# A two-layer Perceiver kernel on one core: which PSUM banks attention, state space preparation and gate of layer 1 use, and two batches' attention outputs in one tile

## The chip, the cores and the metric

The kernel runs on one core of a Trainium2 chip. A core has a matrix engine (TensorE, PE in the profile; its weight loads are PEld), a vector engine (VectorE, DVE), an activation engine (ScalarE, ACT), a general engine (GpSimd, POOL) and a queue that issues transfers (SyncE, SP). They run side by side, each through its own instruction list in a fixed order, and wait for one another by semaphores. Matrix results go to PSUM, which this kernel divides into eight banks of 128 partitions by 512 float32 values.

The metric is the device time of one execution in microseconds. Before the change it is 2087.88 us, the median of three runs (2087.57 to 2094.29).

## The reference

64 sequences of 32 tokens of width 256 attend to 64 contexts of 257 rows of width 256 and go through two layers:

```
x = x + L0_xattn(layernorm(x), ctx)     # attention over the context
x = x + L0_attn(layernorm(x))           # a recurrence (RWKV) and a channel mix
x = x + L0_ffn(layernorm(x))            # 8 experts, two chosen by gates
x = x + L1_xattn(layernorm(x), ctx)     # grouped attention, quantized linear maps
x = x + L1_attn(layernorm(x))           # a selective state space model
x = x + L1_ffn(layernorm(x))            # 8 experts, all summed
```

The change touches the fourth line and the fifth, and through shared banks the sixth. Attention of layer 1 has 16 query heads and 8 key heads of 16:

```
q = bit_linear(x, wq);  k = bit_linear(y, wk);  v = bit_linear(y, wv)
attn = softmax(q k^T / 4);  out = layernorm(attn v);  return bit_linear(out, wo)
```

`bit_linear` normalizes rows, rounds them to 8 bits and multiplies by weights of -1, 0 or 1 with a scale. The state space model is

```
xz = x @ in_proj.T + b;  x_main, z = split(xz)
xc = silu(causal_conv(x_main));  ssm = xc @ x_proj.T + b     # B (16), C (16), delta
h = exp(A dt) * h + dt * B * xc;  y = <h, C> + D * xc         # step by step
out = layernorm((y * silu(z)) @ out_proj.T + b + x)
```

## The kernel before

The 2048 tokens are cut into four blocks (0 to 3) of 512 tokens, which is 16 sequences; a block has four query tiles of 128 tokens, that is of four sequences ("batches") of 32. Each layer part is a stage, a Python function that emits the instructions of one block. `_stage0`, `_stage1` and `_stage2` are layer 0; `_stage3` is attention of layer 1; `_stage4` the state space model, in three functions `ahead` (preparation), `gates` (the silu of z) and `recur` (the recurrence); `_stage5` the experts of layer 1. `layers` (lines 1195 to 1254) calls them in an order in which blocks overlap: beside `recur(b)` of block b stand attention of block b+1 and experts of block b-1. A scheduler below the kernel then puts the instructions of each engine into one fixed list, guided by the order of calling and by its own estimate of times; it also decides which buffer of a pool a tile gets, when the tile is first used.

**The PSUM pools.** While layer 1 runs, the banks are shared out like this: `k.ps` (tag "s") two banks for attention, `k.psh` two for the recurrence (`h`, `outps`), `k.psp` (tag "p") one for preparation and gate, `k.psu` (tag "u") one for the experts' `up`, `t_ps`, `lg_ps` and `rT`, and two which first belong to the experts of layer 0 and then to the sums `acc` of the experts of layer 1. A tile that needs a bank waits until every reader of the bank's last tile is done. Attention of block 0 is called before the pools `psh`, `psp` and `psu` are opened (lines 1225 and 1230).

**Attention, one query tile** (`attend`, line 766). The quantized queries are transposed (`xqT_ps`, L776, copied at L778), multiplied by the weights (`q_ps`, L781, scaled on VectorE at L783), and transposed again (`qT_ps`, L800) into `qm` (L804), which has one buffer. `last_ps` (L787, L789) and `sl_ps` (L807) treat the 257th context row. Then the four batches go in pairs (e = 0 and 2):

- `keys(e)`: `kT_ps` (L823) and `v_ps` (L830) for two batches, evacuated and scaled on VectorE (L825, L836).
- `scores(e, h0)`: for two head pairs at a time two tiles `sc` (L844), their negated maxima `nm` on VectorE (L849, L851), exponentials on ScalarE (L855) with sums.
- `sums(e)`: for one batch, two tiles `pt_ps` of four transposes each (L868), copied on ScalarE (L870), then 16 small matmuls into `oT_ps` (L878). Its two halves are masked and added into `od` by ScalarE (L882) and VectorE (L883).
- `back()`: the weights of the sums (`rt_ps` L904), the output transposed (`po_ps` L916, VectorE L918) and the 257th row added (`vl_ps` L920, L922, GpSimd L923).

`block` (line 703) interleaves them: `keys(e)`, `scores(e, 0)`, then `sums` of both batches of the pair before, then `scores(e, 2)`. All these tiles take turns in the two banks of `k.ps`. At the block's end stand a layer norm (L743, L744 on GpSimd), quantization (L344 to L350), and for each query tile `yqT_ps` (L758) and `wo_ps` (L763), which is added into x at L764.

**State space model.** `ahead` normalizes x, transposes it (`tps`, L123), projects each of four channel groups (`inps`, L976) to ScalarE (L994, L997) and VectorE (L1001, the convolution), then `ssm_ps` (L1012), whose rows go to DRAM and come back broadcast to all partitions (L1016, L1018); softplus gives dt (L1022 to L1030). `gates` has four more `inps` tiles with a silu (L1038). `recur` has for each of 16 states and four channel groups an exponential on ScalarE (L1060), a scan on VectorE (L1061) and a product (L1062); GpSimd makes the scan's inputs (L1056) and adds up y (L1063) for two groups at once, multiplies by the gate (L1066) at the end; then `outps` (L1074).

**Experts of layer 1.** For each of 8 experts: four `up` tiles (L1167) with their evacuation (L1169), one gelu (L1171), and matmuls into `acc` (L1175). Weights are loaded by SyncE (L1162, L1163) into two buffers. The two `acc` tiles leave at L1180, are transposed (`rT`, L1187) and scaled (L1188). In the order of TensorE the experts of one block begin with `t_ps` (L1121) and the gate logits `lg_ps` (L1126).

The small helpers by which the stages take their banks:

```
700    def ps(shape, name, dt=F32):                     # attention
701        return k.ps.tile(shape, dt, name=name, tag="s")
967    def pp(shape, name):                             # preparation and gate
968        return k.psp.tile(shape, F32, name=name, tag="p")
1102   def ps(shape, name):                             # experts
1103       return k.psu.tile(shape, F32, name=name, tag="u")
```

Of the kernel before, what the change touches and what calls it, by code (L numbers as in the profile page):

```python
# [70 lines left out]
def _chan(k, name, j=0):  # L71
    at = CHAN_AT[name] + j
    return k.chan[:, at : at + 1]
# [595 lines left out]
def _stage3(k, w, tmp):  # L669
# [30 lines left out]
    def ps(shape, name, dt=F32):  # L700
        return k.ps.tile(shape, dt, name=name, tag="s")

    def block(b):
        xs = [k.x[b][:, j, :] for j in range(4)]
# [16 lines left out]
        for u in range(9):  # L721
            j, e = divmod(2 * u, 4)
            if u < 8:
                if e == 0:
                    tiles[j] = attend(4 * b + j, j, xq, dq, o4)
                tiles[j].keys(e)
                tiles[j].scores(e, 0)
            if u:
                last, le = tiles[(u - 1) // 2], (2 * u - 2) % 4
                last.sums(le)  # L730
                last.sums(le + 1)
            if u < 8:
                tiles[j].scores(e, 2)
            if u and le == 2:
                last.back()
# [30 lines left out]
    def attend(g, j, xq, dq, o4):  # L766
# [6 lines left out]

        xqT_ps = ps([P, 2, P], "xqT_ps", BF16)
        for c in range(2):
            nc.tensor.transpose(xqT_ps[:, c, :], xq[:, j, c * P : (c + 1) * P], k.identb)  # L776
        xqT = k.wk3.tile([P, 2, P], BF16, name="xqT", tag="xqT")
        nc.scalar.copy(xqT, xqT_ps)  # L778
        q_ps = ps([P, D], "q_ps")
        for c in range(2):  # L780
# [3 lines left out]

        last_ps = ps([P, P + 4], "last_ps")
        for c in range(2):
# [10 lines left out]
        )  # L797
        qT_ps = ps([P, 2, 4, T], "qT_ps")
        for h in range(2):
# [3 lines left out]
        for l in range(2):  # L803
            nc.vector.tensor_scalar(qm[:, :, l].rearrange("p e n g -> p g e n"), qT_ps, half[:, l : l + 1], None, ALU.mult)  # L804
        sl_ps = ps([P, 4, 4], "sl_ps")
        for e in range(4):
# [11 lines left out]
        def keys(e):  # L818


            kT_ps = ps([P, 2, 2 * P], "kT_ps")
            for c in range(2):
                nc.tensor.matmul(kT_ps, wkv[:, c, 0:P], cq[:, c, e : e + 2, 0 : 2 * P], start=c == 0, stop=c == 1)  # L823
            kTs[e] = k.wk3.tile([P, 2, 2 * P], F32, name="kT", tag="kT")
            nc.vector.tensor_tensor(kTs[e], kT_ps, kb[:, e : e + 2, 0 : 2 * P], ALU.mult)  # L825
            v_ps = ps([P, 2, 2, P], "v_ps")
            for m in range(2):
                for f in range(2):
                    for c in range(2):
                        nc.tensor.matmul(  # L830
                            v_ps[:, m, f, :], cq[:, c, e + f, m * P : (m + 1) * P], wkv[:, c, P : 2 * P],
                            start=c == 0, stop=c == 1,
                        )
            vs[e] = k.wk3.tile([P, 2, 2, P], F32, name="v", tag="v")
            cd = k.cdq[:, :, g].rearrange("p (m e) -> p m e", m=2)[:, :, e : e + 2]
            nc.vector.tensor_tensor(vs[e], v_ps, cd.unsqueeze(3).to_broadcast([P, 2, 2, P]), ALU.mult)  # L836
# [23 lines left out]
        def sums(e):  # L860
            e0, f = e - e % 2, e % 2
            pts = []
            for hp in range(2):

                pt_ps = ps([P, 2, 2, P], "pt_ps")
                for h in range(2):
                    for m in range(2):
                        nc.tensor.transpose(pt_ps[:, h, m, :], ws[e0, hp][:, f, h, m * P : (m + 1) * P], k.ident)  # L868
                pt = k.wk3.tile([P, 2, 2, P], F32, name="pt", tag="pt")
                nc.scalar.copy(pt, pt_ps)  # L870
                pts.append(pt)

            oT_ps = ps([P, 2, 2 * T], "oT_ps")
            ob = oT_ps.rearrange("p l q -> p (l q)")
            for m in range(2):
                for h in range(4):
                    r = slice(32 * h, 32 * h + 32)
                    nc.tensor.matmul(  # L878
                        ob[r], vs[e0][:, m, f, r], pts[h // 2][:, h % 2, m, :],
                        start=m == 0, stop=m == 1, skip_group_check=True,  # L880
                    )
            nc.scalar.activation(od4[:, e], oT_ps[:, 0], AF.Copy, scale=half[:, 0:1])  # L882
            nc.vector.scalar_tensor_tensor(od4[:, e], oT_ps[:, 1], half[:, 1:2], od4[:, e], ALU.mult, ALU.add)  # L883

# [49 lines left out]
def _stage4(k, w, wk):  # L934
# [32 lines left out]
    def pp(shape, name):  # L967
        return k.psp.tile(shape, F32, name=name, tag="p")

# [64 lines left out]
    def gates(v):  # L1034

        v.zs = wk.tile([P, C, BT], F32, name="zs", tag="zs", bufs=1)
        for c in range(C):
            nc.scalar.activation(v.zs[:, c, :], project(v, C + c, pp), AF.Silu, bias=_chan(k, "L1_attn_in_proj_b", C + c))  # L1038

# [155 lines left out]
def layers(k, out):  # L1195
# [140 lines left out]
```

## Time and profile before

| what | value |
|---|---|
| time, median of 3 runs | 2087.88 us |
| the profiled execution's own time | 2087.24 us |
| its span, first to last instruction | 2085.2 us |
| TensorE busy | 1597.6 us (77%) |
| VectorE busy | 1384.2 us (66%) |
| GpSimd busy | 1049.5 us (50%) |
| ScalarE busy | 944.1 us (45%) |
| granted TensorE clock, mean | 0.832 |

The span in 40 equal slices of 52 us, each digit the busy share of an engine in tenths (9 is 90% or more), below them the clock that TensorE was granted in tenths of full speed:

```profile
PE   4776967667979788657387789877888787787798
DVE  4588585765485568888777888775787844877100
ACT  2454352303445264434136466447566536564232
POOL 5344646413121324668724677732677843999100
PEclk9676968778989989657697789988699997899799
```

Layer 0 fills the slices up to about the ninth, with attention of block 0 up to the fourteenth. The runs of 8 in VectorE's row with 6 to 7 in GpSimd's are recurrence and attention beside each other; the dips between them are preparations. The run of 9 in GpSimd's row is the last recurrence, and the last three slices are experts alone.

In the views shown later a group of instructions is told by line, engine, operation, tiles ("out<-in"), shape and count. A row of the timeline starts with the start and the duration in us and ends, in brackets, with the idle time of the engine before it and what ended it; a row of the waits names who waited for whom, the total in us, the times and the longest.

### The profile page before, as it was taken

What the parts mean: (1) busy time and instruction counts of PE and PEld (TensorE: products, weight loads), DVE (VectorE), ACT (ScalarE), POOL (GpSimd) and SP (SyncE); (2) the same over time, 40 slices, a digit from 0 to 9 for tenths busy, and PEclk for the clock granted to TensorE, in tenths of its full rate; (3) what the DMA queues carried; (4) which work ended last, traced back from release to release, by engine and by line L of the source; (5) the groups of instructions that cost most, each with busy time, mean ns of one, the idle gap of its engine ahead of it and who ended that gap; (6) DMA issues with size and microseconds to landing.
All of it is one profiled execution on the core that took longest, in us unless ns stands there. A gap on an engine that the chain in (4) does not pass through costs nothing. (4 is left out here: it accounts for less than half of the span.)

```text
span 2085.2 us, 20012 instructions
## 1 busy us (share of the span) xinstructions
PE 1597.6 (77%) x6323; PEld 812.4 (39%) x6323; DVE 1384.2 (66%) x2443; ACT 944.1 (45%) x2001; POOL 1049.5 (50%) x1069
## 2 busy tenths in 40 slices
PE   4776967667979788657387789877888787787798
PEld 3333534334545434433144344433344433233343
DVE  4588585765485568888777888775787844877100
ACT  2454352303445264434136466447566536564232
POOL 5344646413121324668724677732677843999100
PEclk9676968778989989657697789988699997899799
DMA  6754333300001010122002232102222212342121
GB/s 221 228 189 141 102 109 104 100 4 21 21 21 42 20 47 21 51 59 63 10 15 83 66 106 86 46 21 87 71 81 71 52 31 77 87 115 72 39 81 41
DMA packets 88376, 151.23 MB, mean 73 GB/s; under 512 B 7740, under 2 KB 52300, under 8 KB 86224
## 3 DMA queue, kind: packets, MB, share of 16 engines
q1 hardware_dynamic: 85428, 148.75, 23.4%
q10 hardware_dynamic: 2844, 1.22, 0.2%
q8 instruction: 50, 0.82, 0.2%
q14 instruction: 54, 0.44, 0.1%
HBM read 139.03 MB, written 10.92 MB: 72 GB/s over the span
## 5 line engine op out<-in xcount | busy, mean ns | idle before, releaser
L1056 POOL TENSOR_TENSOR g<-dtx,bc 128x1024 f32<-128x1024 f32 x128 | 300.4, 2352 | 191.4 <-DVE h L1061 101.7
L1061 DVE TENSOR_TENSOR_SCAN h<-h,g 128x512 f32<-128x512 f32 x256 | 308.1, 1219 | 47.0 <-ACT h L1060 28.7
L1063 POOL TENSOR_TENSOR xc<-xc,hc 128x1024 f32<-128x1024 f32 x128 | 301.0, 2354 | 34.5 <-DVE hc L1062 29.5
L1167 PE MATMUL up<-xT,w 128*128 128x512 f32 x512 | 288.4, 678 | 33.1 <-ACT hid L1169 29.6
L1175 PE MATMUL acc<-hid,w 128*128 128x512 f32 x512 | 258.0, 624 | 19.9 <-ACT hid L1171 19.9
L1060 ACT ACTIVATE h<-dt,A 128x512 f32<-128x512 f32 x256 | 173.9, 692 | 173.5 <-DVE hc L1062 172.3
L1062 DVE TENSOR_TENSOR hc<-h,bc 128x512 f32<-128x512 f32 x256 | 170.1, 681 | 5.8 <-POOL xc L1063 3.0
L1169 ACT ACTIVATE hid<-up,chan 128x512 f32<-128x512 f32 x128 | 87.2, 681 | 179.2 <-PE up L1167 179.2
L855 ACT ACTIVATE p<-sc,nm 128x256 f32<-128x256 f32 x256 | 117.7, 471 | 95.3 <-DVE nm L851 90.5
L1167 PEld LDWEIGHTS up<-xT,w 128*128 128x128 f32 x512 | 97.7, 209 | 157.3 <-issue 84.6
L630 PE MATMUL weps<-we,xT 128*128 128x512 f32 x256 | 140.0, 671 | 23.3 <-DVE x L632 14.7
L868 PE MATMUL pt_ps<-ident,p 128*128 128x128 f32 x512 | 95.9, 325 | 73.6 <-ACT p L855 36.3
L1175 PEld LDWEIGHTS acc<-hid,w 128*128 128x128 f32 x512 | 96.5, 199 | 137.8 <-issue 99.3
L844 PE MATMUL sc<-kT,qm 32*128 32x256 f32 x512 | 133.9, 447 | 4.9 <-DVE kT L825 2.4
L849 DVE TENSOR_REDUCE nm<-sc 128x2 f32<-128x512 f32 x128 | 86.2, 686 | 56.1 <-PE sc L844 55.1
L868 PEld LDWEIGHTS pt_ps<-ident,p 128*128 128x128 f32 x512 | 67.3, 163 | 123.0 <-ACT p L855 79.1
L89 POOL TENSOR_TENSOR rs_t<-rs_r 128x4 f32<-128x4 f32 (+3 forms) x138 | 33.3, 243 | 160.4 <-DVE rs_r L87 142.5
L844 PEld LDWEIGHTS sc<-kT,qm 32*128 32x128 f32 x512 | 82.7, 207 | 62.6 <-issue 10.8
L1188 DVE SCALAR_TENSOR_TENSOR o<-rT,gt,x 128x256 f32<-128x256 f32 x16 | 7.7, 483 | 133.2 <-PE rT L1187 124.0
L870 ACT COPY pt<-pt_ps 128x512 f32<-128x512 f32 x128 | 74.2, 588 | 32.9 <-PE pt_ps L868 32.3
L1044 POOL TENSOR_TENSOR dtx<-xc,dt 128x2048 f32<-128x2048 f32 x4 | 18.0, 4502 | 138.9 <-DVE dt L1030 127.4
L247 POOL TENSOR_TENSOR cT<-cT,scb 128x2056 f32<-128x2056 f32 x16 | 73.2, 4572 | 25.8 <-PE scT_ps L237 11.5
(389 smaller groups left out, 3166.0 us busy)
## 6 DMA issues: line engine op xcount, KB each, us to landing
bc<-rows SPq DMA_DIRECT2D x64, 512.0 KB
w<-in_L_ffn_w_dram SPq DMA_DIRECT2D x64, 512.0 KB
cT<-in_ctxT_dram SPq DMA_DIRECT2D x16, 1028.0 KB
cq<-cq SPq DMA_DIRECT2D x32, 514.0 KB
cn<-in_ctx_dram SPq DMA_DIRECT2D x64, 256.0 KB
scb<-scales SPq DMA_DIRECT2D x16, 514.0 KB
kb<-steps SPq DMA_DIRECT2D x16, 514.0 KB
x<-in_x_dram SPq DMA_DIRECT2D x4, 512.0 KB
```

The costliest lines, as they stand in the source:

```text
L630: nc.tensor.matmul(ps, xT[:, c, r], we[:, c, e : e + 2, :], start=c == 0, stop=c == 1)
L844: nc.tensor.matmul(sc[h][:, f, :], qm[r, e + f].rearrange("p l n g -> p (l n g)"), kTs[e][r, f, :], start=True, stop=True,)
L855: nc.scalar.activation(w_[:, f, h - h0, :], sc[h][:, f, :], AF.Exp, bias=nm[:, e + f, h : h + 1], accum_out=sm[:, e + f, h : h + 1],)
L868: nc.tensor.transpose(pt_ps[:, h, m, :], ws[e0, hp][:, f, h, m * P : (m + 1) * P], k.ident)
L1056: nc.gpsimd.tensor_tensor(g, dtx[:, c2 : c2 + 2], bc[:, 0:1, :].to_broadcast([P, 2, BT]), ALU.mult)
L1060: nc.scalar.activation(h, dt, AF.Exp, scale=A[:, c2 + c, n : n + 1])
L1061: nc.vector.tensor_tensor_scan(h, h, g[:, c, :], 0.0, ALU.mult, ALU.add)
L1062: nc.vector.tensor_tensor(hc[:, c, :], h, bc[:, 1, :], ALU.mult)
L1063: nc.gpsimd.tensor_tensor(y[:, c2 : c2 + 2], y[:, c2 : c2 + 2], hc, ALU.add)
L1167: nc.tensor.matmul(u, w1[e][:, c, q * P : (q + 1) * P], xT[:, c, :], start=c == 0, stop=c == 1)
L1169: nc.scalar.activation(hid[e][:, q, :], u, AF.Identity, bias=b1)
L1175: nc.tensor.matmul(acc[o], w2[e][:, q, o * P : (o + 1) * P], hid[e][:, q, :], start=n == H, stop=n == E * H + H - 1)
```

## The change

Four things change.

1. A helper `pk` takes a tile from `k.psp` (one bank) if that pool is open, else from `k.ps`. The tiles `xqT_ps`, `q_ps`, `last_ps`, `qT_ps`, `sl_ps`, `kT_ps` and `v_ps` of attention use it. `k.psp` is set to None before block 0, so block 0 keeps them in `k.ps`.
2. `sums(e)` treats both batches of a pair. They share one tile `oT_ps` in one bank, and one instruction of ScalarE and one of VectorE, on twice the columns, move both to `od`.
3. The preparation `ahead` takes its tiles (`tps`, `inps`, `ssm_ps`) from the two banks of `k.ps`.
4. `gates` takes its tiles from the experts' bank `k.psu`.

```diff
+    def pk(shape, name, dt=F32):
+        return k.psp.tile(shape, dt, name=name, tag="p") if k.psp else ps(shape, name, dt)
...
                 last.sums(le)
-                last.sums(le + 1)
...
-        xqT_ps = ps([P, 2, P], "xqT_ps", BF16)
+        xqT_ps = pk([P, 2, P], "xqT_ps", BF16)
...
-        q_ps = ps([P, D], "q_ps")
+        q_ps = pk([P, D], "q_ps")
...
-        last_ps = ps([P, P + 4], "last_ps")
+        last_ps = pk([P, P + 4], "last_ps")
...
-        qT_ps = ps([P, 2, 4, T], "qT_ps")
+        qT_ps = pk([P, 2, 4, T], "qT_ps")
...
-        sl_ps = ps([P, 4, 4], "sl_ps")
+        sl_ps = pk([P, 4, 4], "sl_ps")
...
-            kT_ps = ps([P, 2, 2 * P], "kT_ps")
+            kT_ps = pk([P, 2, 2 * P], "kT_ps")
...
-            v_ps = ps([P, 2, 2, P], "v_ps")
+            v_ps = pk([P, 2, 2, P], "v_ps")
...
         def sums(e):
-            e0, f = e - e % 2, e % 2
-            pts = []
-            for hp in range(2):
-                pt_ps = ps([P, 2, 2, P], "pt_ps")
...
-            oT_ps = ps([P, 2, 2 * T], "oT_ps")
-            ob = oT_ps.rearrange("p l q -> p (l q)")
...
-            nc.scalar.activation(od4[:, e], oT_ps[:, 0], AF.Copy, scale=half[:, 0:1])
-            nc.vector.scalar_tensor_tensor(od4[:, e], oT_ps[:, 1], half[:, 1:2], od4[:, e], ALU.mult, ALU.add)
+            oT_ps = ps([P, 2, 2, 2 * T], "oT_ps")
+            for f in range(2):
+                pts = []
+                for hp in range(2):
+                    pt_ps = ps([P, 2, 2, P], "pt_ps")
...
+                ob = oT_ps[:, f].rearrange("p l q -> p (l q)")
...
+            o2 = od4[:, e : e + 2]
+            nc.scalar.activation(o2, oT_ps[:, :, 0], AF.Copy, scale=half[:, 0:1])
+            nc.vector.scalar_tensor_tensor(o2, oT_ps[:, :, 1], half[:, 1:2], o2, ALU.mult, ALU.add)
...
     def pp(shape, name):
-        return k.psp.tile(shape, F32, name=name, tag="p")
+        return k.ps.tile(shape, F32, name=name, tag="s")
+
+    def pz(shape, name):
+        return k.psu.tile(shape, F32, name=name, tag="u")
...
-            nc.scalar.activation(v.zs[:, c, :], project(v, C + c, pp), AF.Silu, bias=_chan(k, "L1_attn_in_proj_b", C + c))
+            nc.scalar.activation(v.zs[:, c, :], project(v, C + c, pz), AF.Silu, bias=_chan(k, "L1_attn_in_proj_b", C + c))
...
+    k.psp = None
     with left0:
```

The matmuls and the transfers are the same in number and size; 32 instructions of ScalarE and 32 of VectorE go (64 of each become 32, of twice the columns). The scheduler makes new instruction lists for every engine.

More of the change, by code (lines that the diff above doesn't have):

```diff
@@ L860, in sums @@
         def sums(e):
-            e0, f = e - e % 2, e % 2
-            pts = []
-            for hp in range(2):
-                pt_ps = ps([P, 2, 2, P], "pt_ps")
[L866 to L871, printed above, removed]
-            oT_ps = ps([P, 2, 2 * T], "oT_ps")
-            ob = oT_ps.rearrange("p l q -> p (l q)")
[L875 to L883, printed above, removed]
+            oT_ps = ps([P, 2, 2, 2 * T], "oT_ps")
[3 more added lines that the diff above has]
+                    pt_ps = ps([P, 2, 2, P], "pt_ps")
+                    for h in range(2):
+                        for m in range(2):
+                            nc.tensor.transpose(pt_ps[:, h, m, :], ws[e, hp][:, f, h, m * P : (m + 1) * P], k.ident)
+                    pt = k.wk3.tile([P, 2, 2, P], F32, name="pt", tag="pt")
+                    nc.scalar.copy(pt, pt_ps)
+                    pts.append(pt)
+                ob = oT_ps[:, f].rearrange("p l q -> p (l q)")
+                for m in range(2):
+                    for h in range(4):
+                        r = slice(32 * h, 32 * h + 32)
+                        nc.tensor.matmul(
+                            ob[r], vs[e][:, m, f, r], pts[h // 2][:, h % 2, m, :],
+                            start=m == 0, stop=m == 1, skip_group_check=True,
+                        )
+            o2 = od4[:, e : e + 2]
+            nc.scalar.activation(o2, oT_ps[:, :, 0], AF.Copy, scale=half[:, 0:1])
+            nc.vector.scalar_tensor_tensor(o2, oT_ps[:, :, 1], half[:, 1:2], o2, ALU.mult, ALU.add)
         def back():
```

## The prediction

> **What bounds the kernel now.** I read the table of forty slices first: no engine is full for long, and what is busy changes with the stage. So I cut the span where a query block's attention ends (last L764), where a recurrence starts (first L1061) and where it ends (last L1074), and took the view of busy time by stretch:
>
> ```profile
> core 0: us, PE busy (x) PEld busy (x) DVE busy (x) ACT busy (x) POOL busy (x), PEclk, DMA share, GB/s
> 792.00:1044.00 252.00, 150.92 (x748) 84.82 (x748) 213.47 (x350) 92.79 (x243) 170.34 (x114) 0.67 0.16 42
> 1120.00:1378.00 258.00, 207.68 (x880) 103.90 (x880) 207.55 (x328) 142.14 (x290) 177.96 (x134) 0.84 0.22 67
> 1451.00:1691.00 240.00, 192.70 (x818) 95.85 (x819) 187.46 (x300) 131.76 (x274) 174.97 (x133) 0.84 0.22 62
> 1752.00:1923.00 171.00, 132.24 (x290) 56.37 (x290) 137.70 (x161) 94.84 (x120) 156.01 (x84) 0.89 0.30 83
> 1923.00:2086.00 163.00, 138.00 (x320) 60.62 (x318) 13.69 (x47) 47.75 (x52) 12.83 (x44) 0.89 0.18 55
> ```
>
> The first three rows are attention of blocks 1, 2, 3 beside the recurrence of blocks 0, 1, 2 (and, from 1120 on, experts of blocks 0 and 1): VectorE is busy 78 to 85%, TensorE 60 to 80%, neither full. The fourth is the last recurrence, where GpSimd is busy 91% (156.0 of 171). The fifth is experts alone, bound by TensorE. Between the rows stand the state space preparations (1044 to 1120, 1378 to 1451, 1691 to 1752). The chain of waits agrees for the end (its largest entries are experts' matmuls L1175 and L1167) but reaches back only to 1648 us, so for the middle I read waits. VectorE's, from 792 to 1691 us:
>
> ```profile
> DVE nm L849 <- PE sc L844: 41.4, 36, 4.7
> DVE od L883 <- ACT od L882: 18.8, 7, 10.0
> DVE h L1061 <- ACT h L1060: 15.2, 16, 5.3
> DVE kT L825 <- PE kT_ps L823: 14.5, 10, 3.9
> ```
>
> VectorE is idle 197 us of these 899 (701.9 busy), and three of the four largest waits are for attention's PSUM tiles. Why these are late, the timeline shows where one query tile ends and the next begins:
>
> ```profile
> 1511.21 0.48 ACT L855 ACTIVATE p<-sc,nm 128x256 f32<-128x256 f32 x1
> ...
> 1513.81 0.28 PE L776 MATMUL xqT_ps<-identb,xq 128*128 128x128 bf16 x2
> ...
> 1517.80 0.46 DVE L783 TENSOR_SCALAR q<-q_ps,dq 128x256 f32<-128x256 f32 x1
> ...
> 1520.32 0.95 PE L807 MATMUL sl_ps<-klm,qm 128*128 128x4 f32 x8
> ...
> 1522.98 1.89 PE L844 MATMUL sc<-kT,qm 32*128 32x256 f32 x6
> ```
>
> From the last exponential (done 1511.8) to the next scores (1523.0) are 11.2 us in which queries and keys pass through the two banks that scores and transposes also need.
>
> **The change, part by part.** Sums are made against the profiled execution: span 2085.2, its own time 2087.24, so 2.0 us lie around the span; it stands 0.6 below the median of 2087.88. Where instructions go I take from the order of both built programs, engine by engine; no time comes from there.
>
> *Queries and keys in their own bank.* It holds for blocks 1 to 3; block 0 runs before the bank exists. In the new order the next tile's xqT and q stand before the scores' end, and keys of the second half tile right behind those of the first. So the 11.2 us shrink to what the order forces (qm has one buffer, so L804, sl and kT still follow the last scores): 0.9 + 1.0 + 0.6 + 0.7 by their rows and a VectorE turn or two of 1.2 us (L1061), some 5 us, beside the exponentials. At the half tile 4.2 us (1545.2 to 1549.4) lose the keys' 2.5. That takes 8 to 9 us off attention's chain per query tile, some 100 us for twelve. Most of it cannot be cashed: recurrence shares VectorE, whose work between landmarks is the same in both orders (from the first to the last scan 822 us before, 818 after, by mean durations). Only idle time can go, and of it what waits for attention's tiles: 41.4 + 18.8 + 14.5, with q, v and qm (1.9, 2.8, 1.5) 80.9 us. Ends: none of it, all of it. I take half, since nm will still wait for some scores: **-40**.
>
> *One output tile for two batches.* L882 and L883 run half as often on twice the columns. Rows: L882 0.31 us at 64 columns, L855 0.47 at 256, so about 0.36 at 128; L883 0.28, L918 0.41, so about 0.32. For the 24 pairs of blocks 1 to 3, VectorE saves 24 x (0.56 - 0.32) = 6 us. The fourth transpose group no longer waits for L883 of the first batch but for the copy L870 (0.6 us) in the one bank that the output leaves free; the tile is taken only at its first matmul, so the first two groups still have two banks. Beside the waits already counted: **-4** (ends 0 and -6). Block 0 gets this too, but from 480 to 713 us TensorE idles only 31 of 233 us: nothing, from -6 to +6.
>
> *Preparation in two banks, gate in the experts' bank.* Before, each inps tile waits for its eviction, and experts fill in between. After, the four stand in a row. The matmuls from the last wo (L763) to the last ssm (L1012) come, by mean durations per line, to 35.4, 38.3, 36.7 us for blocks 1, 2, 3 before and 32.3, 34.5, 31.1 after; block 3's interval is 34.3 us in the trace (1690.1 to 1724.4), so TensorE sets it. **-12** (0 to -18 with block 0's -5.8). The gate's four tiles of a block now take turns with the experts' up tiles; both orders finish a gate before the experts of the block after it, and y needs it only at L1066. ScalarE loads four tables fewer (4 x 1.28 us), covered by its slack (ScalarE busy 50% from 792 to 1691): 0. The rows and dt loads stand before the expert weights that would block SyncE's queue (w1 and w2 of expert 7 of the block then running), so it is not stalled.
>
> *What is moved.* The experts lag. Of block 2's 128 expert matmuls (each two passes), 13 stand behind the last outps before (2 up, 11 acc), **54** after (22 and 32). The recurrence covered them; in the tail nothing does:
>
> ```profile
> 1928.68 7.13 PE L1175 MATMUL acc<-hid,w 128*128 128x512 f32 x16 [2.28 <-ACT hid L1171]
> ...
> 1948.96 3.58 PE L1126 MATMUL lg_ps<-w_L_ffn_gate_wT,xT 128*128 128x8 f32 x16 [0.68 <-ACT xT L1122]
> 1952.83 3.78 PE L1167 MATMUL up<-xT,w 128*128 128x512 f32 x4 [0.28 <-DVE lg L1136]
> ...
> 1966.51 1.98 PE L1167 MATMUL up<-xT,w 128*128 128x512 f32 x4 [0.78 <-ACT hid L1169]
> ```
>
> Block 3's experts begin only when block 2's output has left (single bank, single xn5 buffer), 17 us after the last acc (1935.8 to 1952.5). So 41 x 0.86 us (four passes in 1.72 in the steady part of the chain) = **+35** go in whole; ends +30 and +40.
>
> *The clock.* 1953 to 1966 us ran at a granted 0.51, after 13 us of thin work; then 1.00. The Trainium skill (TensorE: Matmul & The Clock Gate, Part 1) says that idleness halves the clock and that some 3.4 us of work restore it; here 13 us were needed. By that rule, taking experts' matmuls out of the attention stretches speaks against the change: without experts the clock was 0.67 (792 to 1044), with them 0.84. Attention's matmuls are some 86 us per block by my sums; at 0.67 instead of 0.84, 22 us more for each of two blocks. By the order, 86 of 100 expert matmuls stay beside block 2's attention and 71 of 92 beside block 3's, nearer the row with experts: I take 0, and up to +20 for the range.
>
> Sum: -40 - 4 - 12 + 35 = -21, that is **2066 us**.
>
> **Rivals.** *The tail decides (slower).* Attention's chain gets shorter, but VectorE's fixed order puts scans before nm and kT, so waits only change names; a recurrence's own floor is GpSimd's 150 us (32 L1056 and 32 L1063 at 2.35). From a gain of under 35 us before the last outps on, the 54 matmuls win: with -12 from the preparation and 0 to -10 from attention, 2087 + 35 - 17 = 2105. For it: 80% of VectorE is taken already. Against: the 80.9 us of waits for exactly these tiles.
>
> *Gain and tail cancel.* Attention gives only a quarter (-20): 2087 - 20 - 4 - 12 + 35 = 2086.
>
> *The single bank is too narrow (slower).* Seven tiles take turns there, each waiting for an evacuation behind scans; if a tile's queries come out 4 us later than with two banks, 12 x 4 = 48: 2087 + 48 - 16 + 35, less what idle VectorE time hides, about 2120. The order, which puts keys ahead of need, speaks against it.
>
> *It does not do what it says:* true for block 0 alone, counted at nothing.
>
> **How the numbers follow.** This kernel's measurement tells 0.3% (6 us) from no change. Forecast 0.49 (its own range 2042 to 2080), cancelling 0.13, tail 0.32, narrow bank 0.06. Faster 0.49, same 0.13, slower 0.38. The range is 2042 to 2112: below, three quarters of the 80.9 us and all of the preparation's 18; above, the tail's case with its upper end and a little of the clock.
>
> **What would show it.** Right: waits of kT for kT_ps near zero and of od under 9 us from 792 to 1691; scores within 7 us of the last exponential at a tile's end; the last outps near 1866 and block 3's lg 65 us behind it, not 30. Wrong: the last outps after 1887 (then slower), or kT and q waiting longer than before, or a granted clock under 0.75 in the second and third stretch.

## The result and the profile after

The changed kernel takes 2093.53 us (median of 20 runs, 2085.45 to 2105.28) against 2087.42 us for the kernel before (20 runs, 2077.87 to 2094.29): ratio 1.0038, 95% interval 1.0020 to 1.0055. It is **slower by 0.4%** (0.3% by the medians alone), where 2066 us was forecast (range 2042 to 2112). The profiled execution has a span of 2093.2 us (2085.2 before) and a mean granted clock of 0.835 (0.832).

Landmarks of the two traces, in us from the start (ends of instructions; from one execution each, so differences under some 5 us are not read):

| landmark | before | after | difference |
|---|---|---|---|
| attention of block 0 done | 712.7 | 720.9 | +8.2 |
| recurrence 0, last scan | 1026.1 | 1017.7 | -8.4 |
| attention of block 2 done | 1378.2 | 1347.3 | -30.8 |
| recurrence 2, first and last scan | 1451.2, 1654.7 | 1413.1, 1646.2 | -38.1, -8.5 |
| attention of block 3 done | 1691.0 | 1660.0 | -31.0 |
| last outps (block 3) | 1922.1 | 1899.7 | -22.4 |
| lg of block 3 | 1952.8 | 1964.3 | +11.5 |
| end | 2085.2 | 2093.2 | +7.9 |

By the last outps 22 us are won, but the stretch from there to lg grows from 31 us to 65. At the first scan of recurrence 2 the gain was 38 us. At its last scan 8.5 were left, since that recurrence takes 233 us, not 203; attention of block 3 beside it kept 31. The busy time by stretch in the changed kernel, cut at the same events (attention beside recurrence 0, 1, 2; the last recurrence; experts alone):

```profile
core 0: us, PE busy (x) PEld busy (x) DVE busy (x) ACT busy (x) POOL busy (x), PEclk, DMA share, GB/s
792.00:1036.50 244.50, 153.25 (x767) 87.89 (x766) 216.16 (x337) 93.87 (x237) 170.49 (x114) 0.65 0.17 44
1105.00:1347.00 242.00, 200.32 (x903) 100.75 (x896) 211.05 (x336) 138.55 (x283) 178.78 (x146) 0.87 0.26 74
1413.00:1660.00 247.00, 187.15 (x829) 96.00 (x828) 198.22 (x298) 137.31 (x279) 169.17 (x114) 0.85 0.23 60
1727.00:1900.00 173.00, 120.94 (x266) 51.87 (x265) 143.48 (x164) 96.41 (x120) 156.23 (x84) 0.86 0.28 82
1900.00:2094.00 194.00, 169.92 (x404) 75.45 (x402) 14.23 (x48) 57.16 (x63) 12.84 (x44) 0.94 0.19 57
```

The first two stretches are shorter (252 and 258 before), with VectorE at 88 and 87%. The third is longer (240 before), the last by 31 us (163 before), with 404 instructions of TensorE where 320 were. The clock has not moved where attention runs.

VectorE's waits from 792 to 1691 us in the changed kernel (who waited for whom: total us, times, longest):

```profile
DVE nm L852 <- PE sc L847: 38.2, 22, 14.7
DVE h L1068 <- ACT h L1067: 23.4, 21, 7.4
...
DVE kT L828 <- PE kT_ps L826: 5.5, 4, 2.1
...
DVE od L887 <- ACT od L886: 0.2, 1, 0.2
```

od has gone from 18.8 to 0.2 us and kT from 14.5 to 5.5. nm has 38.2 (41.4 before), but 24.7 of these are three waits from 1372 to 1411, before the first scan of recurrence 2. h now waits 23.4 us for ScalarE's exponential (15.2). The end of a query tile, in the timeline of the changed kernel:

```profile
1540.67 0.48 ACT L858 ACTIVATE p<-sc,nm 128x256 f32<-128x256 f32 x1
...
1542.54 0.95 PE L810 MATMUL sl_ps<-klm,qm 128*128 128x4 f32 x8
...
1544.29 0.60 PE L826 MATMUL kT_ps<-cq,b_L_xattn_wkvT 128*128 128x512 bf16 x2
...
1546.56 1.13 PE L847 MATMUL sc<-kT,qm 32*128 32x256 f32 x8
```

From the last exponential's end (1541.2) to the next scores are 5.4 us; over the nine tile ends inside blocks 1 to 3 the mean is 5.2 us, 11.0 before. The chain did get shorter as described. The tail, TensorE's timeline:

```profile
1940.17 7.13 PE L1182 MATMUL acc<-hid,w 128*128 128x512 f32 x16 [1.00 <-ACT hid L1178]
1947.23 0.33 PE L1194 MATMUL rT<-ident,res 128*128 128x128 f32 x1
...
1960.47 3.58 PE L1133 MATMUL lg_ps<-w_L_ffn_gate_wT,xT 128*128 128x8 f32 x16 [0.68 <-ACT xT L1129]
1964.34 3.78 PE L1174 MATMUL up<-xT,w 128*128 128x512 f32 x4 [0.28 <-DVE lg L1143]
1968.90 1.98 PE L1174 MATMUL up<-xT,w 128*128 128x512 f32 x4 [0.78 <-ACT hid L1176]
```

Block 2's experts run until 1947, 48 us behind the last outps (14 before), and then the same gap of 17 us follows. Block 3 itself then takes 128.9 us from lg to the end instead of 132.4: only its first up tile has the 3.8 us of a low clock (0.56 from 1964 to 1969), where before three had. So the clock gave back 3.5 us that no part of the change was meant to bring.

What had not been foreseen stands in ScalarE's timeline of the last recurrence:

```profile
1760.81 1.28 ACT L1045 ACT_TABLE_LOAD   x1
1764.21 0.69 ACT L1045 ACTIVATE zs<-inps,chan 128x512 f32<-128x512 f32 x1 [2.11 <-PE inps L983]
1764.91 1.28 ACT L1067 ACT_TABLE_LOAD   x1
1766.21 0.69 ACT L1067 ACTIVATE h<-dt,A 128x512 f32<-128x512 f32 x1
1766.92 1.28 ACT L1045 ACT_TABLE_LOAD   x1
1768.21 0.69 ACT L1045 ACTIVATE zs<-inps,chan 128x512 f32<-128x512 f32 x1
1768.92 1.28 ACT L1067 ACT_TABLE_LOAD   x1
1770.21 0.69 ACT L1067 ACTIVATE h<-dt,A 128x512 f32<-128x512 f32 x1
```

The gate zs of block 3 runs almost 40 us into its own recurrence, after the outputs of block 1's experts (1760.7), whose bank it shares, and between each two gates one exponential squeezes in, with a table load before either. In recurrences 2 and 3 all four gates now lie between the first and the last exponential of the recurrence (one of four before). Yet recurrence 3 is hardly longer than before: from the end of its first scan to that of its last are 157 us, 156 before. Between 1760 and 1780 one scan alone waits for an exponential:

```profile
1775.01 1.23 DVE L1068 TENSOR_TENSOR_SCAN h<-h,g 128x512 f32<-128x512 f32 x1 [0.96 <-ACT h L1067]
```

### The profile page after: what moved, and what is told of

The parts are those of the page before. It is cut to its first block, busy times and chain, and to the rows that moved or that the text cites. A ratio compares the mean times of both kernels' runs of the same rounds, so it can differ in the third digit from the quotient of the medians.

```text
span 2093.2 us, 19902 instructions
## 1 busy us (share of the span) xinstructions
PE 1603.1 (77%) x6323; PEld 819.8 (39%) x6323; DVE 1391.9 (66%) x2411; ACT 933.6 (45%) x1965; POOL 1055.9 (50%) x1069
## 5 line engine op out<-in xcount | busy, mean ns | idle before, releaser
L1174 PE MATMUL up<-xT,w 128*128 128x512 f32 x512 | 281.3, 664 | 47.3 <-ACT hid L1176 44.4
L1070 POOL TENSOR_TENSOR xc<-xc,hc 128x1024 f32<-128x1024 f32 x128 | 301.2, 2356 | 24.6 <-DVE hc L1069 19.8
L1067 ACT ACTIVATE h<-dt,A 128x512 f32<-128x512 f32 x256 | 173.8, 691 | 175.5 <-DVE hc L1069 174.8
L630 PE MATMUL weps<-we,xT 128*128 128x512 f32 x256 | 144.5, 688 | 21.9 <-DVE x L632 12.3
L847 PE MATMUL sc<-kT,qm 32*128 32x256 f32 x512 | 135.1, 461 | 19.8 <-DVE od L887 6.9
L530 POOL TENSOR_TENSOR kk<-kk 128x512 f32<-128x512 f32 x32 | 34.1, 1072 | 114.2 <-ACT kk L529 111.3
L881 PE MATMUL oT_ps<-pt,v 128*32 128x128 f32 x1024 | 74.1, 310 | 19.6 <-ACT pt L875 18.9
```

What stands on the lines that cost most here:

```text
L630: nc.tensor.matmul(ps, xT[:, c, r], we[:, c, e : e + 2, :], start=c == 0, stop=c == 1)
L847: nc.tensor.matmul(sc[h][:, f, :], qm[r, e + f].rearrange("p l n g -> p (l n g)"), kTs[e][r, f, :], start=True, stop=True,)
L1067: nc.scalar.activation(h, dt, AF.Exp, scale=A[:, c2 + c, n : n + 1])
L1070: nc.gpsimd.tensor_tensor(y[:, c2 : c2 + 2], y[:, c2 : c2 + 2], hc, ALU.add)
L1174: nc.tensor.matmul(u, w1[e][:, c, q * P : (q + 1) * P], xT[:, c, :], start=c == 0, stop=c == 1)
```

## The experiments

The theory at the start: the gain on the chain is real, and the experts' lag takes it back. "Behind" is the number of block 2's expert matmuls behind the last outps by the built order (13 before, 54 after). Medians and ratios to the kernel before, with 95% intervals; landmarks from one trace each.

| run | what | behind | last outps | to lg | median | ratio |
|---|---|---|---|---|---|---|
| e1_sums | before + merged sums | 9 | 1904.5 | 29.2 | 2067.2 | 0.9914 (0.9888, 0.9939) |
| e2_banks | after, sums per batch | 54 | 1905.0 | 64.6 | 2101.1 | 1.0068 (1.0047, 1.0090) |
| h1_prep | before + preparation in two banks | 0 | 1927.8 | 24.3 | 2085.1 | 0.9994 (0.9979, 1.0010) |
| f1_keys | after, preparation and gate back | 8 | 1936.4 | 28.9 | 2099.0 | 1.0056 (1.0035, 1.0077) |
| f6_keys_s | after, queries and keys back | 13 | 1905.2 | 32.4 | 2073.9 | 0.9934 (0.9914, 0.9954) |
| i1_v_s | after, v back | 38 | 1904.0 | 50.8 | 2087.1 | 1.0001 (0.9987, 1.0015) |
| g1_swap | after, one call moved | 22 | 1908.2 | 37.1 | 2080.1 | 0.9966 (0.9948, 0.9984) |
| e4_after_tail | after, three banks at the end | 39 | 1898.4 | 50.3 | 2074.7 | 0.9942 (0.9922, 0.9961) |
| g2_sums_tail | e1, three banks at the end | 0 | 1922.3 | 22.9 | 2064.6 | 0.9892 (0.9870, 0.9914) |
| e3_gate_s | after, gate in attention's banks | 48 | 1885.8 | 60.3 | 2082.2 | 0.9974 (0.9961, 0.9987) |
| i4_gate_s_sums | e3, queries and keys back | 8 | 1923.0 | 28.9 | 2084.8 | 0.9999 (0.9983, 1.0014) |
| j2_repaired | all four parts, repaired | 7 | 1893.0 | 27.5 | 2047.4 | 0.9831 (0.9807, 0.9856) |
| k1_rep_keys | j2, queries and keys back | 0 | 1926.9 | 22.9 | 2075.9 | 0.9952 (0.9935, 0.9969) |
| k2_rep_sums | j2, sums per batch | 7 | 1893.1 | 27.5 | 2045.6 | 0.9816 (0.9783, 0.9849) |
| k3_rep_gate | j2, gate in experts' bank | 7 | 1907.4 | 27.4 | 2068.6 | 0.9909 (0.9879, 0.9938) |

### Merged sums alone, banks alone

e1_sums is the kernel before with the new `sums(e)` and one call instead of two; e2_banks the changed kernel with the old `sums` and both calls:

```diff
-                last.sums(le)
-                last.sums(le + 1)
+                last.sums(le)
```

> The kernel before with one part of the change: one output tile for two batches; all banks as before. By the built order 9 expert matmuls of block 2 stand behind the last outps (13 before, 54 after). Theory 1 (the experts' lag decides, and it comes from the bank moves): no lag here, merged sums worth a few us: 2079 to 2087, last outps 1915 to 1922, block 3's lg 31 us behind it. Rival (the merged sums cost block 0 its 8 us, since the fourth transposes wait for one bank): attention of block 0 ends 8 us late and the end is 2091 to 2096.

> The changed kernel with its bank moves (queries and keys, preparation, gate), but output tiles per batch as before. 54 expert matmuls stand behind the last outps, as in the changed kernel. Theory 1: the lag comes from here, lg of block 3 is 62 to 68 us behind the last outps, end 2090 to 2098. Rival (merged sums cost 8 us in block 0): block 0's attention ends as before (712) and the end is 2082 to 2087. Rival (merged sums carry the gain of attention): the last outps is near 1915 and the end is 2105 to 2112.

Merged sums alone are faster by 0.9%, far more than expected; block 0's attention does end at 716.6 with them (713.5 with banks alone, 712.7 before), but nothing behind it is late. The banks alone are slower by 0.7%, and the lag is theirs: lg is 64.6 us behind the last outps, to the tenth as in the changed kernel. Both move the last outps by 17 us, and together only by 22. Why, the groups of TensorE's transposes of p show, in the kernel before, e1_sums, e2_banks and the changed kernel (busy, mean ns | idle time before them, and what ended it):

```profile
L868 PE MATMUL pt_ps<-ident,p 128*128 128x128 f32 x512 | 95.9, 325 | 73.6 <-ACT p L855 36.3 <-DVE h L1061 18.3 <-DVE od L883 17.2
```

```profile
L869 PE MATMUL pt_ps<-ident,p 128*128 128x128 f32 x512 | 88.7, 306 | 30.3 <-ACT p L854 14.7 <-DVE h L1061 11.8 <-ACT pt L871 3.7
```

```profile
L872 PE MATMUL pt_ps<-ident,p 128*128 128x128 f32 x512 | 93.3, 317 | 40.0 <-ACT p L859 17.2 <-DVE h L1068 10.0 <-DVE od L887 9.6
```

```profile
L873 PE MATMUL pt_ps<-ident,p 128*128 128x128 f32 x512 | 94.5, 321 | 25.0 <-ACT p L858 13.8 <-ACT pt L875 6.3 <-DVE h L1068 5.0
```

Either part alone removes 34 to 43 of the 73.6 us that TensorE waits there, and the second adds 5 to 15: they pay for the same waits.

### Preparation alone, and three ways to undo a bank

h1_prep is the kernel before with the preparation's helper changed, the gate keeping its bank:

```diff
     def pp(shape, name):
-        return k.psp.tile(shape, F32, name=name, tag="p")
+        return k.ps.tile(shape, F32, name=name, tag="s")
```

> The kernel before with one part of the change: the state space preparation takes its tiles from attention's two banks; the gate stays in the bank it had, queries and keys and output tiles as before. No expert matmul of block 2 stands behind the last outps (13 before). Theory (preparation gains 12 us on the chain, and 13 matmuls leave the tail, 11 us): last outps 1905 to 1915, end 2060 to 2072. Rival A (the four tiles in a row gain nothing, as VectorE's and ScalarE's work on each follows anyway): last outps 1917 to 1925, end 2072 to 2080. Rival B (the preparation takes banks from attention beside it): last outps above 1925, end 2080 to 2095.

Rival B's case: the last outps is later than before, and the time no different. From the last wo add to the last ssm of blocks 1 to 3 are 96.0 us instead of 112.2, so the preparation itself is faster by 16, but attention of block 3, beside it in the same two banks, takes 338 us instead of 313 and ends 19 us later than before.

f1_keys is the changed kernel with `pp` and `pz` both on `k.psp`:

```diff
     def pp(shape, name):
-        return k.ps.tile(shape, F32, name=name, tag="s")
+        return k.psp.tile(shape, F32, name=name, tag="p")
     def pz(shape, name):
-        return k.psu.tile(shape, F32, name=name, tag="u")
+        return k.psp.tile(shape, F32, name=name, tag="p")
```

> The changed kernel with preparation and gate back in the bank they had, which queries and keys now share with them. Only 8 expert matmuls of block 2 stand behind the last outps. Theory 1 (the gain is there and the lag takes it back): last outps 1900 to 1912, lg 31 us behind it, end 2065 to 2077. Rival A (attention's waits only change names; the 22 us before the last outps come from the preparation): last outps 1918 to 1924, end 2083 to 2089. Rival B (one bank for queries, keys, preparation and gate is too narrow): end above 2093.

Rival B: three users in one bank are too many; 2099, without the lag. f6_keys_s gives queries and keys back to attention's banks, i1_v_s only v:

```diff
-        return k.psp.tile(shape, dt, name=name, tag="p") if k.psp else ps(shape, name, dt)
+        return ps(shape, name, dt)
```

```diff
-            v_ps = pk([P, 2, 2, P], "v_ps")
+            v_ps = ps([P, 2, 2, P], "v_ps")
```

> The changed kernel without the bank of queries and keys: these pass through attention's two banks as before, while output tiles for two batches, preparation and gate stay as changed. 13 expert matmuls of block 2 stand behind the last outps, as before the change. Theory 2 (merged sums bring the gain; the bank of queries and keys brings the lag and almost nothing else): lg of block 3 is 29 to 32 us behind the last outps, which is at 1893 to 1904 (1904.5 with merged sums alone, less up to 12 for the preparation); end 2052 to 2065. Rival A (that bank does bring attention's gain in the changed kernel): last outps 1908 to 1922, end 2068 to 2085. Rival B (preparation or gate, in their new banks, stand in attention's or the experts' way): end above 2075 with the last outps or lg late.

> The changed kernel with one of the seven tiles, v, back in attention's two banks; the other six stay in the bank of queries and keys. 38 expert matmuls of block 2 stand behind the last outps (54). In the changed kernel TensorE waits 25 us at v for the evacuation of kT from the same bank. Theory S (the single bank keeps attention's gain small): no such wait, last outps 1885 to 1896, lg 50 to 53 us behind it, end 2065 to 2079. Rival (the wait only moves to scores and transposes, attention gains nothing more): last outps 1898 to 1910, end 2079 to 2092.

f6_keys_s: beside the other parts, the bank of queries and keys moves the last outps by only 5.5 us (1905.2 to 1899.7) and costs 32 us behind it (32.4 to 64.6). Its last outps lies 1.2 us outside the theory's range and lg 0.4, but the time lies in rival A's: the span is 2068.3, and the median another 5.6 us above it. Without this bank the changed kernel is 20 us faster. i1_v_s is the rival's case: the bank that seven tiles share does make v wait for kT's evacuation, as TensorE's waits of the changed kernel from 792 to 1691 us show,

```profile
PE v_ps L833 <- DVE kT L828: 25.4, 13, 4.2
```

but taking v out only moves the wait: v's group then idles 1.5 us, and the scores' group 27.6 instead of 19.8.

### The lag

g1_swap moves one call, e4_after_tail and g2_sums_tail let the experts of blocks 2 and 3 use the two banks that attention no longer needs:

```diff
+            s5(b - 1)
             if b + 2 < NBLK:
                 s3(b + 2)
-            s5(b - 1)
```

```diff
     def ps(shape, name):
+        turn[0] += 1
+        if k.tail and turn[0] % 3:
+            return k.ps.tile(shape, F32, name=name, tag="s")
         return k.psu.tile(shape, F32, name=name, tag="u")
...
+            k.tail = b == NBLK - 1
             s5(b - 1)
```

> The changed kernel with one call moved: the experts of block 0 are called before attention of block 3 instead of behind it, so that the scheduler ranks them higher. By the built order 22 expert matmuls of block 2 stand behind the last outps instead of 54. Theory (the lag is a matter of order, at 0.83 us each): last outps within 5 us of 1899.7, lg 36 to 40 us behind it instead of 64.6, end 2062 to 2072. Rival (what experts get earlier, attention loses; TensorE's time in the third stretch is full): last outps 1910 to 1925, end 2080 to 2095.

> The changed kernel, with the experts' tiles of blocks 2 and 3 taking turns in attention's two banks as well, which are free by then; 39 expert matmuls of block 2 stand behind the last outps instead of 54. Theory 1 (the tail decides, and with it the one bank through which up tiles pass): last outps 1895 to 1903 as in the changed kernel, then 15 matmuls less (13 us), the gap of 17 us between the blocks down by 5 to 10, up tiles no longer waiting for hid (5 to 10): end 2060 to 2075. Rival A (TensorE is the bound of the tail, banks don't matter): the 13 us alone, near 2080. Rival B (the tail is bound by ScalarE or the weights' transfers): 2088 to 2096.

> The kernel before with one output tile for two batches, and the experts' tiles of blocks 2 and 3 taking turns in attention's two banks too. No expert matmul of block 2 stands behind the last outps. Theory: from merged sums alone (span 2062.5) 9 matmuls less (7 us), and from the changed kernel with such experts 2 us of the gap between blocks and 5 us of block 3: end 2044 to 2054, faster than both kernels. Rival (experts drawn forward delay the last recurrence, or block 3's start waits on the same chain as before): 2058 to 2067.

The times from the last outps to lg in the table follow the count closely: 8 or 9 behind give 29, 13 give 31 to 32, 22 give 37, 38 give 51, 48 give 60, 54 give 65, so 0.78 us each ((64.6 - 28.9) / (54 - 8)). A matmul behind the last outps thus costs nearly its full time (0.86 us by the rows that the prediction took). The three runs also show what it costs to draw experts forward: in g1_swap the tail is 27.5 us shorter, but the last outps 8.5 later (between theory and rival), so 2080 rather than 2062 to 2072; in g2_sums_tail the last outps is 18 us later than in e1_sums, and the median the same within the spread (the rival's case). In e4_after_tail it is not later, block 3 itself is 5 us faster (128.9 to 123.5 from lg to the end), and the median lands at the upper end of the theory.

### The gate

e3_gate_s is the changed kernel with the gate in attention's banks:

```diff
     def pz(shape, name):
-        return k.psu.tile(shape, F32, name=name, tag="u")
+        return k.ps.tile(shape, F32, name=name, tag="s")
```

> The changed kernel with the gate's tiles in attention's two banks instead of the experts'. In the changed kernel the four gate tiles of blocks 2 and 3 wait for the experts before them and fall into the recurrence they belong to, where ScalarE switches tables for them (4 x 3.3 us). In this order they stand behind a recurrence's last exponential or at its start; 48 expert matmuls of block 2 stand behind the last outps (54). Theory G (those gates make recurrences 2 and 3 longer): recurrence 3, from first to last scan 157 us in the changed kernel, takes 143 to 150, the last outps is at 1880 to 1892, lg 58 to 62 us behind it, end 2069 to 2081. Rival A (the gate does not matter there, DVE is short for other reasons): last outps 1896 to 1905, end 2084 to 2094. Rival B (the gate takes banks from attention): last outps above 1905, end above 2094.

The last outps comes 14 us earlier than in the changed kernel, and recurrence 2 takes 213 us instead of 233; the median falls to 2082, 1 us above theory G's range, although 48 matmuls are behind. But theory G's own test failed: recurrence 3 got longer (161 us, 157 in the changed kernel). Three of its four gates still lie inside it. (Over all 17 traces recurrence 3 takes 142 to 149 us where none of its gates lies inside and 156 to 162 where one to four do; how many makes no difference, and the kernel before had one. Where none lies inside, the experts of block 2 also begin ahead of the recurrence, and else inside it, so the traces don't show that the gates are the reason.) So the 14 us are won ahead of recurrence 3. From the first scan of recurrence 2 to the end of block 3's attention are 239 us instead of 247, and from there to the first scan of recurrence 3 are 58 instead of 67; the other stretches together take 3 us back.

Are table switches the reason? Table loads ahead of the exponentials (L1067) and of the gates (L1045) are fewer, groups of ScalarE from 1390 to 1900 us, the changed kernel and then e3_gate_s:

```profile
L1067 ACT ACT_TABLE_LOAD x18 | 23.1, 1283 | 0.3
...
L1045 ACT ACT_TABLE_LOAD x8 | 10.3, 1283 | 0.1
```

```profile
L1067 ACT ACT_TABLE_LOAD x10 | 12.8, 1283 | 0.2
...
L1045 ACT ACT_TABLE_LOAD x4 | 5.1, 1283 | 0.1
```

The Trainium skill (ScalarE: Activation LUTs, What ACT_TABLE_LOAD costs) prices a switch at 2.66 us, of which 1.28 is the load. The timeline above has the next activation start 1.31 us after the last one's end (1766.90 to 1768.21), so the load alone is what counts here. Some of the loads only pass to other groups; inside recurrences 2 and 3 they fall from 34 to 26, which is 10 us of ScalarE by this trace, and 21 by an estimate from the page's figure. But ScalarE is not full (137 us busy of 247 in the third stretch), and what would reach the chain most directly is scans that wait for exponentials. These waits, in recurrence 2 and then in recurrence 3, are in the changed kernel

```profile
DVE h L1068 <- ACT h L1067: 15.6, 7, 7.4
DVE h L1068 <- ACT h L1067: 11.5, 16, 2.9
```

and in e3_gate_s

```profile
DVE h L1068 <- ACT h L1067: 10.1, 6, 4.1
DVE h L1068 <- ACT h L1067: 16.3, 12, 5.6
```

27.1 and 26.4 us in all: no difference. (In the pair k3_rep_gate and j2_repaired below there are 38 and 26 loads, and 21.2 and 20.5 us of such waits.) So the gate's place costs 14 us, and its table switches are not shown to be why. Another difference is in the order. With its gate late, recurrence 2 in e3_gate_s has its last outps at 1678, when block 3's convolution is done. In the changed kernel it is at 1662, and the layer norm behind it stands ahead of the convolution in VectorE's list. The convolution so starts 17.6 us after attention's end instead of 12.8; the changed kernel and then e3_gate_s:

```profile
1677.59 0.73 DVE L1008 SCALAR_TENSOR_TENSOR xc<-xpad,chan,xc 128x512 f32<-128x512 f32 x1
```

```profile
1667.15 5.23 DVE L1008 SCALAR_TENSOR_TENSOR xc<-xpad,chan,xc 128x512 f32<-128x512 f32 x7 [4.67 <-ACT xc L1004]
```

No run separates this order from the table switches, so the reason stays open.

i4_gate_s_sums takes the bank of queries and keys from e3_gate_s (`pk` as in f6_keys_s).

> The run before the last (changed kernel, gate in attention's banks; last outps at 1885.8) without the bank of queries and keys: these pass through attention's two banks too. 8 expert matmuls of block 2 stand behind the last outps (48 there), and the gates stand behind a recurrence's last exponential. It asks what the bank of queries and keys is worth on the chain when no gate falls into a recurrence. Theory (5 us, as with the gate in the experts' bank): last outps 1888 to 1897, lg 28 to 30 us behind it, end 2046 to 2057. Rival A (the gates had hidden its worth, it is 15 us or more): last outps 1900 to 1912, end 2058 to 2072. Rival B (gate, preparation, queries and keys are too much for two banks): last outps above 1912, end above 2072.

The last outps is 37 us later than in e3_gate_s, which is rival B's case, by the landmark and by the time. Four runs show how much of it is the crowding of the two banks; the time of the last outps:

| | gate in the experts' bank | gate in attention's banks |
|---|---|---|
| queries and keys in attention's banks | 1905.2 (f6_keys_s) | 1923.0 (i4_gate_s_sums) |
| queries and keys in their own bank | 1899.7 (changed) | 1885.8 (e3_gate_s) |

The gate's move to attention's banks costs 18 us where queries and keys are there too, and gains 14 where they are not. (In f6_keys_s no gate of blocks 2 and 3 lies inside its recurrence.) So of the 37 us, 18 are the crowding; the bank itself brings 5.5 us beside a gate in the experts' bank, and 19 if the gate is moved out of its way (1905.2 to 1885.8).

### The repaired kernel, and one part undone at a time

j2_repaired is the changed kernel with the edits of e3_gate_s, g1_swap and e4_after_tail together.

> All four parts of the change with its three costs repaired: gate in attention's two banks, experts of block 0 called before attention of block 3, experts of blocks 2 and 3 in three banks. 7 expert matmuls of block 2 stand behind the last outps. Theory (the change's gain was real and lost to the experts' lag and the gate's place): last outps 1884 to 1898, lg 25 to 29 us behind it, 123 us for block 3: end 2034 to 2050, faster than the kernel before with merged sums and experts in three banks (2064.6). Rival (experts drawn forward cost the chain what they save at its end, as with the call moved alone, where the last outps came 8.5 us later): last outps 1900 to 1912, end 2052 to 2065.

At 2047.4 us it is faster than both kernels, by 1.7% than the one before and by 2.2% than the changed one (2047.42 / 2093.53). The last two stretches of it, the last recurrence and experts alone:

```profile
1718.00:1893.00 175.00, 131.38 (x309) 60.58 (x308) 136.58 (x164) 101.49 (x127) 156.27 (x85) 0.88 0.33 90
1893.00:2043.00 150.00, 127.42 (x311) 58.09 (x309) 14.34 (x48) 43.64 (x49) 12.82 (x44) 0.91 0.17 53
```

Experts alone take 150 us where they took 194 in the changed kernel and 163 before, and the last outps is 29 us earlier than before the change. Made alone, the three repairs bring 11, 13 and 19 us against the changed kernel, together 46. Three runs undo one part each: queries and keys back in attention's banks, sums per batch, gate in the experts' bank (edits as above).

> The repaired kernel (2047.4) without the bank of queries and keys. No expert matmul of block 2 stands behind the last outps (7). Theory A (with no gate in the recurrences that bank is worth some 37 us on the chain): last outps 1915 to 1930, end 2062 to 2076. Rival (it is worth 5 us, as beside a gate in the experts' bank): last outps 1892 to 1902, end 2040 to 2050.

> The repaired kernel with output tiles per batch, as before the change; the same 7 expert matmuls behind the last outps. Theory (merged sums and the banks pay for the same waits, so beside the banks merged sums bring 5 to 8 us, as between the run with bank moves only and the changed kernel): end 2049 to 2057. Rival (they bring 17 to 20 us everywhere, as alone): end 2060 to 2070.

> The repaired kernel with the gate in the experts' bank, as the change puts it; the same 7 expert matmuls behind the last outps, gates 5 to 7 exponentials inside recurrences 2 and 3. Theory (the gate's place costs the chain some 14 us, as in the changed kernel): last outps 1900 to 1912, end 2055 to 2066. Rival (experts that are earlier let the gate through early enough, and it costs nothing): end 2042 to 2051.

Without the bank of queries and keys: 2075.9, 28.5 us slower, the last outps 34 later. As in i4_gate_s_sums, four users then share attention's two banks, so this is not the bank's worth alone. With the gate in the experts' bank: 2068.6, 21 slower (14 between the two traced executions), the last outps 14.4 later; there again all four gates of blocks 2 and 3 lie inside their recurrences. These 14 us arise at other places than in the first pair: 5 by the end of block 2's attention, 9 in attention beside recurrence 2, 5 in recurrence 3, less 5 in the preparation between; only the second is clearly more than one trace can mislead by. With sums per batch: 2045.6, no difference, at odds even with the small gain of the theory. So with the gate in attention's banks, the bank of queries and keys carries the gain, and merged sums are worth nothing beside it; beside the gate in the experts' bank they still bring 7.5 us (e2_banks to the changed kernel).

## Why the prediction was wrong

- **The tail, +35:** right. 33.9 us measured (64.6 - 30.7), and the gap of 17 us stayed.
- **Own bank for queries and keys, -40: one of the two steps that failed.** The mechanism is as described: scores follow 5.2 us behind the last exponential, and the waits that were counted at 80.9 us fell to 48 (38.2 + 0.2 + 5.5, and 2.2 each for qm and v). But half of them was to come out of the chain, and the last outps moved by 5.5 us when this part was added to the others (f6_keys_s to the changed kernel), by 19 with the gate out of the experts' bank as well (e3_gate_s). The waits were no measure of the gain: in e1_sums the same ones are 77.8 us, and the last outps still came 18 us earlier.
- **One oT tile, -4:** as a step beside the others about right (5.3 at the last outps against e2_banks, 0 in the repaired kernel). That alone it would bring 18 us on the chain was not seen: it was costed as instructions saved, not as a bank held half as often.
- **Preparation, -12:** in its own place 9.5 us (102.7 against 112.2 us from wo to ssm). Alone it gave nothing: attention of block 3, in the same banks, took 25 us more (h1_prep). That cost was not in the sum.
- **Gate in the experts' bank, 0: the other step that failed.** The argument was that the gate is done before the experts of the block after it, that y needs it only at the end, and that ScalarE has slack. But the lag that the same text counted at the tail moves the gate as well, which waits for the experts in their bank and so falls into recurrences 2 and 3. That place costs 14 us at the last outps (e3_gate_s against the changed kernel, and k3_rep_gate against j2_repaired). ScalarE's slack did cover the table loads as far as the scans' waits show; by what else the gate's place costs 14 us stays open.
- **The clock, 0:** right (0.87 and 0.85 in the second and third stretch). The 13 us of work that the prediction saw at 0.51 are no fixed cost: the changed kernel has about 5 at 0.56.

Of the 56 us that the chain was to gain, 22 came, with 35 as the point from which the tail decides. The runs account for them in this order: merged sums -17.6 (e1_sums; -4 forecast), preparation and gate +0.7 (f6_keys_s; -12), the bank -19.4 (-40), the gate's place beside that bank +13.9 (0). In another order the shares would be others, since parts pay for the same waits; each is from one trace. With the gate moved, e3_gate_s has the chain at -36 and the kernel at 0.9974. The rival that held is the tail's, by its landmark (last outps after 1887, then slower), but not for its reason: VectorE's idle time up to the last scan did fall, from 550 to 519 us.

## What to carry to other kernels

A bank move is costed for every user of both banks: find what is queued in the bank ahead of a moved tile, and where that will stand once the change has shifted the order, before a step is put at nothing. Where a scheduler fills gaps of one stage with matmuls of another, closing the gaps delays the filler; count what is left behind the last covered point, and move the filler's call or give it the banks that are free by then. And two edits that remove waits at the same tile are not added: run each alone and one undone. If undoing a part also crowds another bank, as with four users in two banks here, run the fourth corner of the table before the difference is called the part's worth.

## What was not expected of the hardware

A switch of ScalarE's tables costs 1.31 us from the end of one activation to the start of the next. Eight of them in a row of gates and exponentials, from 1760 to 1778 us, left VectorE's scans waiting for an exponential for 0.96 us only. With the same matmuls and transfers, banks and order moved the time between 2045.6 and 2101.1 us.
